# Tile by images in a diagonal LSTM kernel: another layout of the resident rows, other engines for the first statistics and the waiting rows' rounds

## The chip, the cores and the metric

The kernel runs on one core of one Trainium2 chip. A core has five engines that run their own instruction streams in order and meet at semaphores: TensorE (PE; PEld is its weight load), VectorE (DVE), ScalarE (ACT), GpSimd (POOL) and SyncE (SP), which here issues most of the DMA transfers. Times are device microseconds of one execution of the whole program; a kernel's time is the median of its runs.

## The reference

Input x has 16 images of 128 channels, 64 rows and 64 columns, in float32. What is computed is two residual layers, each on a group-normalised copy of its input (32 groups of 4 channels, statistics over the image):

```python
x = x + diagonal_lstm(gn(x), w_is, b_is, w_ss, b_ss)
x = x + quantum_conv(gn(x), pre_w, pre_b, q_weights, post_w, post_b)

# diagonal LSTM: row i is shifted right by i, and a scan runs over the 127 shifted columns
def step(h, c, ist):                       # h, c: [B, 128, 64 rows]
    gates = ist + w_ss[:, :, 0] @ h_of_row_above + w_ss[:, :, 1] @ h + b_ss
    o, f, i = sigmoid(gates[:384]); g = tanh(gates[384:])
    c = f * c + i * g
    return o * tanh(c), c
```

`ist` is `w_is @ gn(x) + b_is` on the shifted columns. Outside the image the shifted input is zero, but the state isn't: a row that hasn't begun still runs the recurrence on biases alone, and its state depends only on the step. The quantum layer is a fixed function per pixel: four angles from 128 channels, a simulated circuit of four qubits and two layers, four expectation values, and 128 channels out of these.

## The kernel before, in words

Channels lie on the 128 partitions throughout. The kernel has three stages.

**First stage.** The images are loaded and their statistics taken. Forty of the 64 rows of every image stay in SBUF in `ring`; the other 24 are loaded only for the statistics, into `rest` and `spare` tiles. `ring` is `[P, RING // ROWS, NB, BLOCK]`: blocks of four rows outermost, within a block the 16 images, within an image 256 elements. `rows(b)` loads image b into it by five transfers of 256 KB on SP's queue, `behind(b)` the remaining rows by three. `statistics(b, k)` is one bn_stats over 512 elements on DVE, eight for an image, `aggregated(b)` a bn_aggr of these. Interleaved with the images by a fixed ratio run 33 rounds (`inv_step`, `EARLY = 33`) that compute the state of rows that wait, one after the other: four products of `wsT` with the last state, broadcast to 128 columns (L195), four gate activations with a bias operand (L198), three small products and sums on Pool (L201 to L203), tanh and the product with the output gate on ScalarE (L205, L206). After each round stand two `keep` products (L178), whose results nobody reads. Pool's `turned` and `coefficients` compute the circuit's coefficients before the rounds. After the last round Pool copies the states into `hst` (L399, L400), TensorE computes the first gates' products (L405), three more `keep` products of 384 columns, and then `group_mean` (L143) turns the aggregated statistics into group means; the first normalisation and the scan follow.

**Scan.** Step t (160 steps, `NSTEP`) treats all 16 images along one diagonal of 32 rows; there are two bands of 32 rows, the second 65 steps later. In full steps an operation covers 512 columns: 32 rows of 16 images, held in two halves (q = 0, 1). A step does, on Pool: the copy to `edge` (L873), the differences of two rows' states (L620, L623), the addition of the state to the stored rows (`residual`, L632), and the normalised inputs of step t+2 (`normalised`, L570, L575, L580). TensorE has four wxT products on those inputs (L589) and the products with `wsT`, `w1T` and `w0T` (L768); the w0T products read the differences. DVE and ScalarE do the gates (L783, L787, L818) and the cell (L835 to L853). Where the others have time, DVE takes statistics of finished rows for the second normalisation (`statistics`, L720).

`diagonal` builds the access pattern into `ring`: a block's rows are addressed in pairs, and where the pairs don't align with a block, an operation is split into pieces. When the last column of a block of four rows is done, `residual` sends the block to `low` in DRAM by a transfer of 2 MB (L644), if its place is needed; when DVE has taken its statistics (`statistics`, called earlier in the step than that step's `residual`), the block's place is filled with four rows not yet loaded, by another of 2 MB (L727). There are six of each in the trace, and SP issues both. This stage's instructions are issued in the order in which they are written, under a manual schedule; the waits between them are derived by a framework from the addresses that each one reads and writes.

**Last stage.** Angles, sines, circuit products and outputs go by pieces of 512 pixels of an image; rows that are in `low` are read back. `rows_of(b, k)` gives a piece's place, `finish` adds the output to the rows and sends it out (L1072); in `ring`, two adjacent images share the place of the sum so that a transfer's source is in one stretch.

Of the kernel before, what the change touches and what calls it, by code (L numbers as in the profile page):

```python
# [27 lines left out]
EARLY = 33  # L28
FIRST = 8
# [52 lines left out]
def kernel(  # L82
# [27 lines left out]
    ring = const.tile([P, RING // ROWS, NB, BLOCK], F32, name="ring")  # L110
# [24 lines left out]

    def block(r):

        return (r + AHEAD if r < SLOTS else r - SLOTS) // ROWS
# [18 lines left out]
    with ExitStack() as scan:  # L157
# [29 lines left out]
        def inv_step(j, pool):  # L187


            ps = {}  # L190
            rhs = hinv[:, j : j + 1].to_broadcast([P, P])
            for g in ORDER:
                ps[g] = pool.tile([P, P], F32, name=f"inv_ps{j}_{g}", tag=f"inv{g}")
                w = wsT[:, g * 128 : (g + 1) * 128]
                nc.tensor.matmul(ps[g], lhsT=w, rhs=rhs, start=True, stop=True)  # L195
            ac = small.tile([P, 4], F32, name=f"inv_a{j}", tag="inv_a")
            for g in ORDER:
                nc.scalar.activation(ac[:, g : g + 1], ps[g][:, 0:1], FUNC[g], bias=bias[:, g : g + 1])  # L198
            ig = small.tile([P, 2], F32, name=f"inv_i{j}", tag="inv_i")
            c = cinv[:, j + 1 : j + 2]  # L200
            nc.gpsimd.tensor_mul(ig[:, 0:1], ac[:, GF : GF + 1], cinv[:, j : j + 1])  # L201
            nc.gpsimd.tensor_mul(ig[:, 1:2], ac[:, GI : GI + 1], ac[:, GG : GG + 1])
            nc.gpsimd.tensor_add(c, ig[:, 0:1], ig[:, 1:2])  # L203
            th = small.tile([P, 1], F32, name=f"inv_t{j}", tag="inv_t")
            nc.scalar.activation(th, c, AF.Tanh)  # L205
            nc.scalar.activation(  # L206
                hinv[:, j + 1 : j + 2], th, AF.Identity, scale=ac[:, GO : GO + 1]
            )
# [7 lines left out]
        with ExitStack() as prep:  # L216
# [27 lines left out]
            def rows(b):  # L244
                for k in ORDERED:
                    at = (2 * k * ROWS - AHEAD) * NW if k else SLOTS * NW
                    nc.sync.dma_start(
                        out=ring[:, 2 * k : 2 * k + 2, b, :],
                        in_=xv[b, :, at : at + CHUNK].rearrange("c (k n) -> c k n", n=BLOCK),
                    )  # L250
# [31 lines left out]
            def statistics(b, k):  # L282
                v = ring[:, 2 * k : 2 * k + 2, b, :] if k < 5 else rests[b][k - 5]
                nc.vector.bn_stats(stats[:, b, k, :], v)
# [6 lines left out]

            q3 = qw.rearrange("p (n a) -> p a n", a=3)
            ang = pp.tile([P, 2, 3, 8], F32, name="ang")
# [3 lines left out]
            def turned():  # L297
# [9 lines left out]
                nc.scalar.activation(trig, ang, AF.Sin, scale=TWO_PI)  # L307

            def coefficients():
                nc.gpsimd.tensor_mul(co[:, 0], trig[:, 0, 0, :], trig[:, 0, 2, :])  # L310
                nc.gpsimd.tensor_mul(co[:, 1], trig[:, 1, 0, :], trig[:, 0, 2, :])
                nc.gpsimd.tensor_mul(co[:, 2], trig[:, 0, 1, :], trig[:, 1, 2, :])
                nc.gpsimd.tensor_mul(co[:, 3], trig[:, 1, 1, :], trig[:, 1, 2, :])
                nc.gpsimd.tensor_scalar_mul(co[:, 4:8], co[:, 0:4], -1.0)
                nc.gpsimd.tensor_copy(cur[:, 0], expand)
                nc.gpsimd.memset(cur[:, 1], 0.0)
# [44 lines left out]
            coefficients()  # L361
# [9 lines left out]
            done = 0  # L371
            for b in range(NB):
                while b < NB - 1 and done * (NB - 1) < EARLY * (b + 1):
                    inv_step(done, ps_inv)
                    keep(ps_keep, "keep", ring[:, 2, b, 0:P])
                    keep(ps_keep, "keep", wsT[:, 0:P])
# [7 lines left out]
                    done += 1  # L384
                if b + 2 < NB:
                    rows(b + 2)
                if b + 1 < NB:
                    behind(b + 1)
                    for k in ORDERED:
                        statistics(b + 1, k)  # L390
                for k in (5, 6, 7):
                    statistics(b, k)
                aggregated(b)
# [111 lines left out]
        origin = ring[:, 0, 0, 0:1]  # L505
# [27 lines left out]
        def diagonal(t, band, q, j0, j1):  # L533


            j = j0
            while j < j1:
                odd = (j + AHEAD // 2 * (1 - band)) % 2
                n = 1 if odd or j + 1 == j1 else (j1 - j) // 2 * 2
                r = 2 * j + q + AHEAD * (1 - band)  # L540
                at = r // ROWS * NB * BLOCK + r % ROWS * NW + t - BAND * band - 2 * j - q
                dims = [[BLOCK, NB]]
                if n > 1:
                    dims = [[NB * BLOCK - ROWS, n // 2], [2 * NW - 2, 2]] + dims
                yield j, n, bass.AP(origin.tensor, origin.offset + at, [list(origin.ap[0])] + dims)
                j += n
# [5 lines left out]
        def over(v, n):  # L552
            if n == 1:
                return v
            return v.unsqueeze(1).unsqueeze(1).to_broadcast([P, n // 2, 2, NB])

        def by_pairs(v, q, j, n):
            v = v[:, q, j * NB : (j + n) * NB]
            return v if n == 1 else v.rearrange("p (k h i) -> p k h i", h=2, i=NB)

        def normalised(t):
# [4 lines left out]
            for band in range(2):  # L566
                s0, s1 = slots(t, band)
                j0, j1 = max(0, s0 - 1 + s0 % 2) // 2, (s1 + 1) // 2
                for j, n, x0 in diagonal(t, band, 0, j0, j1):
                    nc.gpsimd.tensor_sub(by_pairs(xn, 0, j, n), x0, over(mean1, n))  # L570
                j0, j1 = s0 // 2, s1 // 2
                uppers = diagonal(t, band, 0, j0, j1)
                for (j, n, lower), (_, _, upper) in zip(diagonal(t, band, 1, j0, j1), uppers):
                    of = over(mean1, n) if plain(t) else upper
                    nc.gpsimd.tensor_sub(by_pairs(xn, 1, j, n), lower, of)  # L575
# [49 lines left out]
        def residual(t, new, engine=nc.gpsimd):  # L625

            for band in range(2):
                s0, s1 = slots(t, band)
                for q in range(2):
                    j0, j1 = (s0 + 1 - q) // 2, (s1 + 1 - q) // 2  # L630
                    for j, n, x1 in diagonal(t, band, q, j0, j1):
                        engine.tensor_add(x1, x1, by_pairs(new, q, j, n))  # L632


            for g in range(NG2):
# [6 lines left out]
                if done == NW:  # L642
                    if 4 * g < NLOW:
                        nc.sync.dma_start(  # L644
                            out=low[:, :, 4 * g * NW : (4 * g + 4) * NW].rearrange("b c n -> c b n"),
                            in_=ring[:, block(4 * g)],
# [61 lines left out]
        def statistics(us):  # L708

            while waiting:  # L710
# [6 lines left out]
                v = ring[:, q, i, :].rearrange("p (r w) -> p r w", w=NW)[:, :, w0:w1]  # L717
                if w1 - w0 == NW:
                    v = ring[:, q, i, :]
                nc.vector.bn_stats(stats[:, i, g - FIRST * k, :], v)  # L720
                if i == NB - 1:
# [4 lines left out]
                    if 4 * g < NLOW:  # L726
                        nc.sync.dma_start(  # L727
                            out=ring[:, q],
# [147 lines left out]
        def low_rows(queue, n, v):  # L876
            b, k = n // NT, n % NT
            of = low[b, :, k * CHUNK : (k + 1) * CHUNK]
            queue.dma_start(out=v, in_=of if len(v.shape) == 2 else of.rearrange("p (k n) -> p k n", n=BLOCK))
# [4 lines left out]
        with tc.manual_schedule():  # L884
# [26 lines left out]
            v = ring[:, block(NH - ROWS)].rearrange("p i (r w) -> p i r w", w=NW)[:, :, :, NW - STRIP :]  # L911
# [17 lines left out]

# [46 lines left out]
    def rows_of(b, k):  # L976
        if k < NT:
            return lows[NT * b + k]
        q = block(2 * ROWS * k)
        return ring[:, q : q + 2, b, :]  # L980

    def half(v, c):
# [3 lines left out]
        return v[:, c] if len(v.shape) == 3 else v[:, c * BLOCK : (c + 1) * BLOCK]  # L986
# [70 lines left out]
    def finish(b, h, po, c=None):  # L1057
        for j in range(4):
# [3 lines left out]
            to = place = v  # L1062
            if c is not None:
                o, to = o[:, c * BLOCK : (c + 1) * BLOCK], x1
            elif k >= NT:


                q = block(2 * ROWS * k)
                to = ring[:, q, b - 1 : b + 1, :] if b % 2 else ring[:, q + 1, b - 2 : b, :]
                y = y.rearrange("p (k n) -> p k n", n=BLOCK)  # L1070
                place = to.rearrange("p k n -> p (k n)")
            nc.vector.scalar_tensor_tensor(to, y, b_out, x1, ALU.add, ALU.add)  # L1072
            nc.sync.dma_start(out=o, in_=to if c is not None else place)
            if c is None or c == 1 and k < NT:
                places.append(place)
# [96 lines left out]
```

## Time and profile before

| | us |
|---|---|
| runs of the kernel before | 1411.84, 1413.09, 1413.08 |
| median | 1413.08 |
| span of the profiled execution | 1411.1 |
| the median over that span | 2.0 |
| first stage, up to group_mean (L143) | 0 to 100.97 |
| scan | about 104 to 1287 |
| last stage | about 1287 to 1411 |
| busy: TensorE, DVE, ScalarE, Pool | 1354.3, 979.7, 777.0, 921.1 |
| moved by DMA | 107.06 MB |

The profile is of one execution. Busy times are of the engine, not of its queue: an engine that waits at a semaphore is not busy. A timeline line has the start in us, the duration (of several joined instructions together), the engine, the line of the kernel, the operation with its output and inputs by tile name, shape and count, and in brackets the idle time ahead of it with what ended it. A line of a table of stretches has the stretch and its length, then for PE, PEld, DVE, ACT and POOL the busy us with the number of instructions, the granted TensorE clock, the DMA share and GB/s.

### The profile page before, as it was taken

What the parts mean: (1) busy time and instruction counts of PE and PEld (TensorE: products, weight loads), DVE (VectorE), ACT (ScalarE), POOL (GpSimd) and SP (SyncE); (2) the same over time, 40 slices, a digit from 0 to 9 for tenths busy, and PEclk for the clock granted to TensorE, in tenths of its full rate; (3) what the DMA queues carried; (4) which work ended last, traced back from release to release, by engine and by line L of the source; (5) the groups of instructions that cost most, each with busy time, mean ns of one, the idle gap of its engine ahead of it and who ended that gap; (6) DMA issues with size and microseconds to landing.
All of it is one profiled execution on the core that took longest, in us unless ns stands there. A gap on an engine that the chain in (4) does not pass through costs nothing. (4 is left out here: it accounts for less than half of the span.)

```text
span 1411.1 us, 20316 instructions
## 1 busy us (share of the span) xinstructions
PE 1354.3 (96%) x6046; PEld 966.1 (68%) x6046; DVE 979.7 (69%) x2541; ACT 777.0 (55%) x1852; POOL 921.1 (65%) x1823
## 2 busy tenths in 40 slices
PE   6778999999999999999999999999999999999995
PEld 4658988777777777666677777776666777886332
DVE  7983565566665666787777776666665566876996
ACT  4545666555555555555555555555555566554331
POOL 4226788777777777777788876777777677773300
PEclk9999999999999999999999999999999999999997
DMA  9980000000000000133333100000000000004999
GB/s 326 367 287 2 1 2 0 1 1 1 0 1 1 0 1 1 60 120 120 120 120 120 60 1 1 0 1 1 1 1 0 1 1 1 2 30 143 386 404 350
DMA packets 78925, 107.06 MB, mean 76 GB/s; under 512 B 5552, under 2 KB 53712, under 8 KB 78816
## 3 DMA queue, kind: packets, MB, share of 16 engines
q1 hardware_dynamic: 74176, 94.39, 19.2%
q0 software_dynamic: 3408, 10.58, 2.0%
q8 instruction: 48, 0.79, 0.2%
q10 hardware_dynamic: 1232, 0.80, 0.2%
q14 instruction: 61, 0.50, 0.1%
HBM read 59.61 MB, written 46.14 MB: 75 GB/s over the span
## 5 line engine op out<-in xcount | busy, mean ns | idle before, releaser
L589 PE MATMUL ps<-spare,wxT 128*128 128x512 f32 (+18 forms) x1280 | 480.6, 519 | 0.0
L783 DVE TENSOR_TENSOR ps<-ps,both 128x256 f32<-128x256 f32 (+9 forms) x536 | 219.5, 411 | 304.4 <-PE ps L768 302.6
L787 ACT ACTIVATE ps<-ps,bias 128x512 f32<-128x512 f32 (+23 forms) x480 | 279.4, 583 | 221.7 <-DVE ps L783 185.2
L768 PE MATMUL ps<-spare,w1T 128*128 128x256 f32 (+16 forms) x1272 | 346.6, 354 | 8.8 <-DVE spare L744 4.6
L589 PEld LDWEIGHTS ps<-spare,wxT 128*128 128x128 f32 x1280 | 231.8, 191 | 172.6 <-issue 155.5
L768 PE MATMUL ps<-spare,w0T 128*128 128x256 f32 (+16 forms) x1272 | 343.8, 352 | 0.8 <-POOL spare L623 0.8
L818 ACT COPY both<-ps 128x256 f32<-128x256 f32 (+9 forms) x536 | 189.8, 356 | 181.1 <-PE ps L768 161.4
L632 POOL TENSOR_TENSOR ring<-ring,spare 128x256 f32<-128x256 f32 (+8 forms) x487 | 247.7, 540 | 30.8 <-DVE stats L720 20.7
L768 PEld LDWEIGHTS ps<-spare,w1T 128*128 128x128 f32 x1272 | 230.4, 190 | 35.8 <-DVE spare L853 6.8
L768 PEld LDWEIGHTS ps<-spare,wsT 128*128 128x128 f32 x1088 | 195.5, 190 | 80.5 <-DVE spare L853 29.9
L768 PE MATMUL ps<-spare,wsT 128*128 128x256 f32 (+14 forms) x1088 | 243.8, 366 | 2.4 <-DVE spare L853 1.2
L768 PEld LDWEIGHTS ps<-spare,w0T 128*128 128x128 f32 x1272 | 230.3, 190 | 22.2 <-POOL spare L623 1.0
L580 POOL TENSOR_TENSOR spare<-spare,rstd 128x512 f32<-128x512 f32 (+10 forms) x160 | 171.0, 1069 | 14.8 <-DVE rstd L154 2.3
L575 POOL TENSOR_TENSOR spare<-ring 128x256 f32<-128x256 f32 (+8 forms) x213 | 147.2, 701 | 0.0
L847 ACT ACTIVATE g<-cst 128x256 f32<-128x256 f32 (+20 forms) x320 | 103.2, 369 | 64.2 <-DVE cst L846 63.3
L570 POOL TENSOR_TENSOR spare<-ring,mean 128x16 f32<-128x16 f32 (+8 forms) x247 | 130.9, 540 | 8.3 <-DVE mean L144 7.2
L853 DVE TENSOR_TENSOR spare<-g,ps 128x256 f32<-128x256 f32 (+17 forms) x319 | 105.7, 368 | 43.3 <-ACT g L847 40.8
L623 POOL TENSOR_TENSOR spare<-spare 128x240 f32<-128x240 f32 (+9 forms) x136 | 102.7, 755 | 29.3 <-DVE spare L853 25.5
L787 ACT ACTIVATE g<-ps,bias 128x512 f32<-128x512 f32 (+20 forms) x160 | 97.4, 609 | 26.9 <-DVE ps L783 20.7
L873 POOL COPY spare<-spare 128x16 f32<-128x16 f32 x64 | 21.1, 330 | 134.2 <-DVE spare L853 134.2
L846 DVE TENSOR_TENSOR cst<-cst,ps 128x256 f32<-128x256 f32 (+20 forms) x320 | 104.6, 368 | 5.5
L843 DVE TENSOR_TENSOR ps<-ps,g 128x512 f32<-128x512 f32 (+20 forms) x160 | 95.1, 595 | 19.0 <-ACT g L787 18.8
(370 smaller groups left out, 1097.3 us busy)
## 6 DMA issues: line engine op xcount, KB each, us to landing
out_dram<-ring SPq DMA_DIRECT2D x93, 256.0 KB, 5.3
ring<-in_x_dram SPq DMA_DIRECT2D x80, 256.0 KB, 5.6
low<-ring SPq DMA_DIRECT2D x6, 2048.0 KB, 7.5
ring<-in_x_dram SPq DMA_DIRECT2D x6, 2048.0 KB, 8.3
spare<-in_x_dram SPq DMA_DIRECT2D x27, 256.0 KB, 5.5
rest<-in_x_dram SPq DMA_DIRECT2D x21, 256.0 KB, 5.6
ring<-low POOLq DMA_DIRECT2D x18, 256.0 KB, 6.7
low<-low POOLq DMA_DIRECT2D x14, 256.0 KB, 5.9
```

The costliest lines, as they stand in the source:

```text
L570: nc.gpsimd.tensor_sub(by_pairs(xn, 0, j, n), x0, over(mean1, n))
L575: nc.gpsimd.tensor_sub(by_pairs(xn, 1, j, n), lower, of)
L580: nc.gpsimd.tensor_mul(v, v, r)
L589: nc.tensor.matmul(ps[g][:, :, a:b], lhsT=wxT[:, g * 128 : (g + 1) * 128], rhs=xns[t % 2][:, :, a:b], start=t > 0, stop=True, skip_group_c ...
L632: engine.tensor_add(x1, x1, by_pairs(new, q, j, n))
L768: nc.tensor.matmul(out, lhsT=w[:, g * 128 : (g + 1) * 128], rhs=rhs, start=False, stop=True, skip_group_check=True,)
L783: nc.vector.tensor_add(v, v, both[g][:, a:b])
L787: nc.scalar.activation(to[:, :, a:w], ps[g][:, :, a:w], FUNC[g], bias=bias[:, g : g + 1])
L818: nc.scalar.copy(both[g][:, a:b], ps[g][:, 0, a:b])
L846: nc.vector.tensor_add(c[:, q], c[:, q], ig[:, q])
L847: nc.scalar.activation(th[:, q, a:w], c[:, q], AF.Tanh)
L853: nc.vector.tensor_mul(new[:, q, a:v], th[:, q, a:v], act[GO][:, q, a:v])
```

## The change

The tile `ring` gets the image as its outermost index: `[P, NB, RING * NW]`. An image's forty rows are one stretch; a diagonal is one operation for each half and band, no longer pieces; an image is loaded by three transfers of 4, 4 and 2 KB per partition instead of five; the sum of the last stage is written in its own place.

In the first stage, the first 512 elements' statistics of images 1 to 8 are taken by two ScalarE passes with an accumulator (`moments_of`: sum of differences to the first element, sum of their squares). The aggregation of images 1 to 12 goes to Pool, as a generator of small operations for four images at a time (`gathering`), of which one portion is issued after each round; what is left follows after the last round. Images 0 and 13 to 15 keep bn_aggr. A round's products have 32 columns instead of 128; the bias is brought by a product of the identity with the broadcast bias, which starts the accumulation, and the activations have no bias operand. The two `keep` products of a round become one of 384 columns. The sines and coefficients of the circuit move behind the rounds and the rest of the aggregation.

```diff
-    ring = const.tile([P, RING // ROWS, NB, BLOCK], F32, name="ring")
+    ring = const.tile([P, NB, RING * NW], F32, name="ring")
...
+    def place(r):
+
+        return (r + AHEAD if r < SLOTS else r - SLOTS) * NW
+
     def block(r):
 
-        return (r + AHEAD if r < SLOTS else r - SLOTS) // ROWS
+        return ring[:, :, place(r) : place(r) + BLOCK]
...
-        def inv_step(j, pool):
+        def inv_step(j, pool, ident):
             ps = {}
-            rhs = hinv[:, j : j + 1].to_broadcast([P, P])
+            rhs = hinv[:, j : j + 1].to_broadcast([P, THIN])
             for g in ORDER:
-                ps[g] = pool.tile([P, P], F32, name=f"inv_ps{j}_{g}", tag=f"inv{g}")
+                ps[g] = pool.tile([P, THIN], F32, name=f"inv_ps{j}_{g}", tag=f"inv{g}")
+                of = bias[:, g : g + 1].to_broadcast([P, THIN])
+                nc.tensor.matmul(ps[g], lhsT=ident, rhs=of, start=True, stop=False)
+            for g in ORDER:
                 w = wsT[:, g * 128 : (g + 1) * 128]
-                nc.tensor.matmul(ps[g], lhsT=w, rhs=rhs, start=True, stop=True)
+                nc.tensor.matmul(ps[g], lhsT=w, rhs=rhs, start=False, stop=True)
...
-                nc.scalar.activation(ac[:, g : g + 1], ps[g][:, 0:1], FUNC[g], bias=bias[:, g : g + 1])
+                nc.scalar.activation(ac[:, g : g + 1], ps[g][:, 0:1], FUNC[g])
...
             def rows(b):
-                for k in ORDERED:
-                    at = (2 * k * ROWS - AHEAD) * NW if k else SLOTS * NW
+                for r, n in ((0, SLOTS // 2), (SLOTS // 2, SLOTS // 2), (SLOTS, AHEAD)):
                     nc.sync.dma_start(
-                        out=ring[:, 2 * k : 2 * k + 2, b, :],
-                        in_=xv[b, :, at : at + CHUNK].rearrange("c (k n) -> c k n", n=BLOCK),
+                        out=ring[:, b, place(r) : place(r) + n * NW],
+                        in_=xv[b, :, r * NW : (r + n) * NW],
                     )
...
+            def moments_of(b):
+                at = place(SLOTS)
+                v, x0 = ring[:, b, at : at + CHUNK], ring[:, b, at : at + 1]
+                junk = ps_small.tile([P, CHUNK], F32, name=f"junk{b}", tag="small")
+                for k, func in enumerate((AF.Identity, AF.Square)):
+                    nc.scalar.activation(
+                        junk, v, func, bias=x0, scale=-1.0, accum_out=sums1[:, k, b : b + 1]
+                    )
+
+            def gathering(b0):
+                b1 = b0 + GATHER
+                pair = [P, GATHER, 2]
+                means, inners = entries[:, b0:b1, :, 1], entries[:, b0:b1, :, 2]
+                s1, s2 = (sums1[:, k, b0:b1] for k in range(2))
+                if b0 in apart:
+                    x0 = ring[:, b0:b1, place(SLOTS)].unsqueeze(2).to_broadcast(pair)
+                    nc.gpsimd.tensor_scalar_mul(s1, s1, -1.0 / CHUNK)
+                    nc.gpsimd.tensor_add(means[:, :, 0:2], s1.unsqueeze(2).to_broadcast(pair), x0)
+                    yield
...
+                def total(to, v):
+                    n = 8
+                    while n > 1:
+                        nc.gpsimd.tensor_add(gathered[:, :, 0:n], v[:, :, 0:n], v[:, :, n : 2 * n])
+                        v, n = gathered, n // 2
+                        yield
+                    nc.gpsimd.tensor_add(to.unsqueeze(2), v[:, :, 0:1], v[:, :, 1:2])
+                    nc.gpsimd.tensor_scalar_mul(to, to, 1.0 / 16)
+                    yield
+
+                yield from total(m, means)
+                nc.gpsimd.tensor_sub(gathered, means, m.unsqueeze(2).to_broadcast([P, GATHER, 16]))
+                nc.gpsimd.tensor_mul(gathered, gathered, gathered)
+                yield
+                nc.gpsimd.tensor_scalar_mul(within, inners, 1.0 / BLOCK)
+                nc.gpsimd.tensor_add(gathered, gathered, within)
+                yield
+                yield from total(var, gathered)
...
+
+            def coefficients():
                 nc.scalar.activation(trig, ang, AF.Sin, scale=TWO_PI)
-
-            def coefficients():
+                nc.scalar.activation(warm, shift, AF.Sqrt)
...
             biases()
-            coefficients()
...
             for b in range(NB):
                 while b < NB - 1 and done * (NB - 1) < EARLY * (b + 1):
-                    inv_step(done, ps_inv)
-                    keep(ps_keep, "keep", ring[:, 2, b, 0:P])
-                    keep(ps_keep, "keep", wsT[:, 0:P])
+                    inv_step(done, ps_inv, ident)
+                    some()
+                    keep(ps_keep, "keep", wsT[:, 0 : 3 * P])
...
+                if b in apart:
+                    moments_of(b)
...
-                        statistics(b + 1, k)
+                        if k or b + 1 not in apart:
+                            statistics(b + 1, k)
...
-                aggregated(b)
+                if b in (0, *range(13, NB)):
+                    aggregated(b)
+                if b in (5, 9, 13):
+                    behind_pool.append(gathering(b - GATHER))
+            for later in behind_pool:
+                for _ in later:
+                    pass
+            coefficients()
...
         def diagonal(t, band, q, j0, j1):
...
+            r = 2 * j0 + q + AHEAD * (1 - band)
+            at = r * NW + t - BAND * band - 2 * j0 - q
+            dims = [[2 * NW - 2, j1 - j0], [RING * NW, NB]]
+            return bass.AP(origin.tensor, origin.offset + at, [list(origin.ap[0])] + dims)
...
-                    for j, n, x1 in diagonal(t, band, q, j0, j1):
-                        engine.tensor_add(x1, x1, by_pairs(new, q, j, n))
+                    if j0 < j1:
+                        x1 = diagonal(t, band, q, j0, j1)
+                        engine.tensor_add(x1, x1, by_pairs(new, q, j0, j1))
...
                             out=low[:, :, 4 * g * NW : (4 * g + 4) * NW].rearrange("b c n -> c b n"),
-                            in_=ring[:, block(4 * g)],
+                            in_=block(4 * g),
...
                         nc.sync.dma_start(
-                            out=ring[:, q],
+                            out=q,
                             in_=xv[:, :, (RING + 4 * g) * NW : (RING + 4 * g + 4) * NW].rearrange(
```

## The prediction, made before the changed kernel had run

> **What bounds the kernel now.** I read the forty slices first, then stretches of the scan, then the order of time in one scan step, and last the first hundred microseconds.
>
> ```profile
> PE   6778999999999999999999999999999999999995
> DVE  7983565566665666787777776666665566876996
> POOL 4226788777777777777788876777777677773300
> PEclk9999999999999999999999999999999999999997
> ```
>
> ```profile
> 700.00:800.00 100.00, 100.00 (x371) 69.76 (x370) 71.82 (x184) 58.94 (x128) 81.08 (x184) 1.00 0.32 106
> ```
>
> A slice is 35 us. DVE leads the first three, TensorE the scan, DVE the end. In the stretch 700 to 800 TensorE is busy all 100 us at full clock and Pool 81: the scan runs at TensorE's pace, so whatever delays a product there is added to the time. What Pool still has spare shows in step 70 (start, us, engine, line):
>
> ```profile
> 610.12 0.20 POOL L873 COPY spare<-spare 128x16 f32<-128x16 f32 x1 [1.65 <-DVE spare L853]
> 610.46 0.86 POOL L623 TENSOR_TENSOR spare<-spare 128x240 f32<-128x240 f32 x1
> 611.29 2.34 POOL L632 TENSOR_TENSOR ring<-ring,spare 128x16 f32<-128x16 f32 x7
> 613.59 0.67 POOL L570 TENSOR_TENSOR spare<-ring,mean 128x192 f32<-128x192 f32 x1
> 615.82 1.27 POOL L580 TENSOR_TENSOR spare<-spare,rstd 128x512 f32<-128x512 f32 x1
> 618.73 0.20 POOL L873 COPY spare<-spare 128x16 f32<-128x16 f32 x1 [1.64 <-DVE spare L853]
> ```
>
> ```profile
> 612.46 0.59 PE L768 MATMUL ps<-spare,w0T 128*128 128x256 f32 x2
> ```
>
> ```profile
> 613.59 0.38 SPq L727 DMA_DIRECT2D ring<-in_x_dram  x1
> 620.79 0.37 SPq L644 DMA_DIRECT2D low<-ring  x1
> ```
>
> The period is 8.61 us (610.12 to 618.73). Pool idles 1.65 of it; its differences end at 611.32 and the first w0T product, which reads them, starts at 612.46, so its lead is 1.14 us more. Behind the differences stand, in Pool's order, the adds to the ring (residual, L632) and the two-steps-ahead normalisation. The page puts the 2 MB reload of a block (L727) at 8.3 us to landing, nearly a whole step, and the copy to low (L644) at 7.5. Neither is waited for in step 70: Pool's only waits from 560 to 780 are 41.0 us for DVE, 25 times.
>
> In the first stage a round of the waiting rows takes 2.39 us, 33 times (hinv starts at 88.98, then 91.38):
>
> ```profile
> 88.98 0.30 ACT L206 ACTIVATE hinv<-inv_t,inv_a 128x1 f32<-128x1 f32 x1
> 89.33 0.97 PEld L195 LDWEIGHTS inv_ps<-hinv,wsT 128*128 128x128 f32 x8 [0.66 <-ACT hinv L206]
> 89.85 0.93 ACT L198 ACTIVATE inv_a<-inv_ps,bias 128x1 f32<-128x1 f32 x4 [0.58 <-PE inv_ps L195]
> 91.38 0.29 ACT L206 ACTIVATE hinv<-inv_t,inv_a 128x1 f32<-128x1 f32 x1
> ```
>
> It is a chain of latencies; its last hinv is written at 94.06. DVE is busy 19.8 of every 20 us there and ends its last aggregation at 100.87; group_mean follows at 100.97. So DVE sets the end of this stage: what follows the rounds, the first gates' products, is over at 96.4.
>
> **What the Trainium skill says.** "DMA: Bandwidth & Descriptors", Anatomy of one DMA: DMA engines do not wait on semaphores, the issuing sequencer does, and about 2 us of a transfer are fixed. So a Pool that waits for a landing waits the whole 8.3 us; the trace agrees on the size (2.1 MB at 350 to 390 GB/s plus 2 is near 8). "TensorE: Matmul & The Clock Gate", LDWEIGHTS: the load's cost goes with the stationary's columns. The trace agrees: fp32 products of 16 and of 128 columns both start 0.22 us apart, so a narrow product is no cheaper to issue. Same page, Part 1: an idle window of about 3.4 us halves the clock until a busy one. The trace has one: sparse products from 99.5 to 102.9, then a granted clock of 0.50 from 103.0 to 106.3. "ScalarE: Activation LUTs", What ACT_TABLE_LOAD costs: a pointer operand adds about 93 ns; here L198 with its bias takes 263 ns, L205 without 203.
>
> **The change, part by part.**
>
> *Ring by images, in the scan.* A diagonal then steps over all images at 10 KB, so the address range of one access spans nearly the whole ring, other blocks' rows included. In the built program's order of instructions with their waits, residual's first add now waits for a block transfer in twelve steps: in steps 70, 74, 78, 82, 86, 90 for the reload issued in that same step, in 68, 72, ... 88 for the copy to low issued the step before. None of these is a true dependency, and the program before has none of them. Behind that add on Pool are the normalisation and the next differences, and for those waits TensorE.
>
> First reload: issue 613.59; landing +8.3; four merged adds instead of seven 1.85 (L570's 64 and 192 columns at 0.34 and 0.67 put 0.17 on a piece, three pieces fewer than 2.34); normalisation 3.5 (0.67+0.84+0.34+0.40+1.27); L873 to L623 1.2. The differences are there 14.9 us after the issue; TensorE wants them at 612.46+8.61 = 621.07, 7.5 after. Stall 7.4. The other five are issued earlier in their step (785.08 against a product at 794.03: 8.95), stall 5.95 each. Sum 7.4 + 29.8 = **37 us**. From below: if landing is 7.5 and Pool catches up half a microsecond, 30. From above, if the reload lands at 9.3: 43.
>
> Each stall is longer than one idle window, so the clock should be half for some 3.4 us after it: 1.7 us lost, six times 10; not each gap holds a full window, I take **9** (0 to 12).
>
> The low copies land 7.5 after the issue, 628.3 in the first case, when Pool gets to the add (8.61 x 2 after 611.3 is 628.5): 0, at most 1 each. The add also waits for the step's statistics in three steps of four from 68 to 98, some 2.2 us each (DVE's group ends at 613.5, Pool is ready at 611.3); Pool's 1.65 idle, 0.5 saved and 1.14 lead cover it: 0, up to 7 us in all. Merged adds shorten Pool, which has time left: 0, and below nothing too no more than that, since TensorE is full.
>
> *First stage.* DVE loses 8 x 0.69 (images 1 to 8) + 12 x 0.372 (aggregations) = 10.0 us and would end near 92. Loads in 4 KB pieces instead of 1 KB: records of 1, 2 and 4 KB take 47, 86 and 159 ns, some 10% less for an image, so the load doesn't hold DVE up. But the cover changes hands:
> - A round's latency falls by 0.18 to 2.2 (0.06 to 0.09 without the pointer; 0.09 by a narrow last pass, since L143's result of 16 columns is read 0.43 us after its product starts, L195's of 128 after 0.52), but TensorE now issues eight products (8 x 0.22) and a 384-column filler (0.6 to 0.7) in it: 2.4, as before. Eight rounds have two ScalarE passes over 512 columns put ahead (about 0.58 each as L787, 0.6 exposed: 5 us). The first round starts 1.9 us earlier, since Sin, coefficients and memsets no longer stand ahead. Last hinv 92.5 to 97, I take 95.
> - Behind the last round Pool still has 27 of the aggregation's small dependent steps (0.2 to 0.4, mean 0.31: 8.4 us), the seven coefficient steps moved there (1.25), three copies (0.5); then TensorE's eight first products (1.8) and three fillers (2.1) stand ahead of group_mean. Sin's table load (1.28) is hidden by the 27 steps. Total 14.1 after the last Pool step of a round, 0.5 before hinv: 94.5 + 14.1 = 108.6.
> So group_mean is at 108.6 against 100.97: **+8** (+5 to +10; DVE's end alone would give -8).
>
> *Last stage.* Same bytes and counts; a sum into 2-D rather than 3-D places takes 741 against 743 ns: 0.
>
> Sum against the profiled 1411.1: +37 +9 +8 = 1465; the median of the runs is 2.0 above the profile, so **1467**. About 0.2% (2.8 us) is what a measurement can tell from no change.
>
> **Rivals.**
> - *The likeliest*, 1467 (1448 to 1484): chance 0.60.
> - *Stalls as said, but DVE and the loads set the first stage's end* (Pool's small steps nearer 0.2 and fit between rounds): 1413 + 46 - 8 = 1451. For it: DVE's 10 us are real. Against: 27 steps stand after the last round in Pool's order. 0.14.
> - *The waits are absorbed*: the transfers land before Pool needs them. Then the scan costs 0 to 10 and the first stage 8: 1425. For it: such a wait costs only what exceeds the 3.3 us of spare and lead. Against: 8.3 us to landing on six reloads. 0.17.
> - *Faster*: the waits cost nothing and DVE's end at 92 to 93 is the stage's end: 1413 - 8 = 1405. It decides once an average round takes below about 2.05 us and landing below about 3 us after issue; the trace shows 2.39 and 8.3. 0.06.
> - *No net effect*: no stall, and the first stage ends as now: 0.03.
>
> The predicted time is the likeliest's, 1467. The range 1424 to 1482 takes most of it, the second, and the upper half of the third. Faster 0.06, same 0.03, slower 0.91.
>
> **What would show it.** Right: Pool's residual waits on DMA in steps 70, 74, ... 90, six holes of 6 to 7 us in TensorE, 34 us apart or a little more, each followed by half clock; group_mean at 106 to 111 behind Pool's gathering. Wrong: TensorE full from 560 to 900, or group_mean before 100.

## The result, and the profile after

The changed kernel takes 1534.75 us (median; 1533.66 to 1547.27) against 1412.82 (the median of four runs of the kernel before): a ratio of 1.0888 (95% interval 1.085 to 1.0926), 122 us slower. The forecast was 1467, with a range to 1482. The direction was right, and so was the mechanism in the scan; the first stage was off by 66 us. (Single executions of four kernels took longer than the others, by some 12 us for the changed kernel and the one with its first stage alone and by 65 to 69 us for the filler kernel and the combined one; the text says which is meant.)

Of the page's slices, now 38 us each, the clock's row shows what the forecast had not:

```profile
PE   7999699999999999998888889999999999999996
PEclk9555799999999999999999999999999999999998
```

The stretches of the first stage (length, then busy us and count of PE, PEld, DVE, ACT, POOL, then clock, DMA share, GB/s):

```profile
20.00:40.00 20.00, 19.66 (x116) 16.59 (x116) 14.94 (x24) 10.94 (x55) 3.49 (x19) 0.80 1.00 377
40.00:60.00 20.00, 20.00 (x77) 17.27 (x77) 17.45 (x29) 8.53 (x36) 2.69 (x14) 0.50 1.04 404
80.00:100.00 20.00, 20.00 (x80) 17.57 (x79) 14.70 (x26) 8.18 (x34) 3.24 (x17) 0.50 0.59 230
120.00:140.00 20.00, 20.00 (x76) 17.19 (x76) 0.00 (x0) 5.40 (x27) 3.78 (x20) 0.50 0.00 0
```

From 31.9 to 159 TensorE is at half clock and, but for short gaps, always busy; then it waits 9.29 us for Pool, and the clock is full again at 171.8. Its instructions in 20 us fall from 116, in a stretch of which 12 us are at full clock, to 77. The kernel before was busy for less than four fifths of such a stretch, at full clock:

```profile
40.00:60.00 20.00, 15.76 (x102) 12.45 (x101) 19.79 (x34) 11.95 (x51) 5.21 (x27) 1.00 1.07 364
```

DVE and the loads are done by 95 (DVE's last aggregation starts at 94.62), and then the core does nothing but rounds and what Pool has left. One round at full clock, and one at half:

```profile
25.64 0.97 PE L201 MATMUL inv_ps<-bias,ident 128*128 128x32 f32 x8
26.45 1.06 PE L204 MATMUL inv_ps<-hinv,wsT 128*128 128x32 f32 x8
27.34 0.89 PE L184 MATMUL I-365_366<-wsT 128*128 128x384 f32 x2
28.07 0.97 PE L201 MATMUL inv_ps<-bias,ident 128*128 128x32 f32 x8
```

```profile
60.43 1.76 PE L201 MATMUL inv_ps<-bias,ident 128*128 128x32 f32 x8
62.00 1.90 PE L204 MATMUL inv_ps<-hinv,wsT 128*128 128x32 f32 x8
63.71 1.63 PE L184 MATMUL I-671_672<-wsT 128*128 128x384 f32 x2
65.13 1.75 PE L201 MATMUL inv_ps<-bias,ident 128*128 128x32 f32 x8
```

From start to start of L201 that is 2.43 us and 4.70. The last hinv is written at 158.6, and group_mean, at 100.97 before, comes here (DVE's line, which reads its result, says how long DVE had waited):

```profile
174.76 0.40 PE L149 MATMUL gm<-mv,wide_sb 128*128 128x16 f32 x2
175.20 0.17 DVE L150 TENSOR_SCALAR mean<-gm 128x16 f32<-128x16 f32 x1 [80.20 <-PE gm L149]
```

The waits in the scan are as forecast. Waits of Pool and of TensorE between 560 and 1000 (us in all, times, longest):

```profile
POOL ring L707 <- DMA ring<-in_x_dram: 59.1, 6, 10.5
POOL ring L707 <- DVE stats L795: 26.4, 17, 2.4
```

```profile
PE ps L843 <- POOL spare L697: 37.0, 6, 7.0
```

And the first of the six holes (the time in which TensorE stands still), in TensorE's timeline and in stretches of it:

```profile
700.97 1.22 PE L843 MATMUL ps<-spare,w0T 128*128 128x256 f32 x2 [7.03 <-POOL spare L697]
701.99 1.06 PE L843 MATMUL ps<-spare,w1T 128*128 128x256 f32 x2
```

```profile
694.00:695.00 1.00, 0.00 (x0) 0.00 (x0) 0.00 (x0) 0.00 (x0) 0.32 (x1) 1.00 0.00 0
702.00:703.00 1.00, 1.00 (x4) 0.81 (x3) 0.43 (x1) 0.23 (x1) 1.00 (x4) 0.50 0.00 0
706.00:707.00 1.00, 1.00 (x3) 0.38 (x2) 1.00 (x3) 0.76 (x2) 0.18 (x1) 1.00 1.05 347
```

By milestones: the scan's first wxT product starts at 178.47 instead of 104.45 (+74.0); from there to the first product on the sums of the second normalisation it is 1227.4 us instead of 1178.3 (+49.1); what follows takes 127.7 instead of 128.4. Together 122.4, the difference of the two spans.

### The profile page after: what moved, and what is told of

The parts are those of the page before. It is cut to its first block, busy times and chain, and to the rows that moved or that the text cites. A ratio compares the mean times of both kernels' runs of the same rounds, so it can differ in the third digit from the quotient of the medians.

```text
span 1533.5 us, 20475 instructions
## 1 busy us (share of the span) xinstructions
PE 1450.9 (95%) x6244; PEld 1051.2 (69%) x6244; DVE 965.7 (63%) x2521; ACT 782.6 (51%) x1886; POOL 898.6 (59%) x1653
## 4 chain that ended last, share of the span: by engine, by line
PE 72%; DVE 4%; DMA 3%; POOL 3%; issue 1%; ACT 1%; DVEq 0%; ACTq 0%; SPq 0%; POOLq 0%
PE ps L843 41%; PE ps L663 24%; DMA ring<-in_x_dram 3%; PE po_None L1121 3%; PE theta_None L1070 2%; PE am_None L1099 1%; POOL ring L707 1%; DVE spare L928 1%; DVE stats L795 1%; DVE ps L918 1%; POOL spare L654 1%; DVE ps L858 1%; POOL spare L649 1%; DVE cst L921 0%; POOL spare L644 0%
## 5 line engine op out<-in xcount | busy, mean ns | idle before, releaser
L843 PE MATMUL ps<-spare,w0T 128*128 128x256 f32 (+16 forms) x1272 | 352.4, 359 | 37.6 <-POOL spare L697 37.6
L843 PE MATMUL ps<-spare,w1T 128*128 128x256 f32 (+16 forms) x1272 | 352.8, 359 | 8.8 <-DVE spare L819 4.8
L707 POOL TENSOR_TENSOR ring<-ring,spare 128x256 f32<-128x256 f32 (+15 forms) x375 | 231.2, 643 | 106.6 <-DMA ring<-in_x_dram 59.1
L843 PEld LDWEIGHTS ps<-spare,w0T 128*128 128x128 f32 x1272 | 234.4, 194 | 62.6 <-POOL spare L697 40.2
L843 PEld LDWEIGHTS ps<-spare,w1T 128*128 128x128 f32 x1272 | 234.9, 194 | 37.6 <-DVE spare L928 6.6
L649 POOL TENSOR_TENSOR spare<-ring 128x256 f32<-128x256 f32 (+13 forms) x165 | 139.6, 846 | 0.0
L922 ACT ACTIVATE g<-cst 128x256 f32<-128x256 f32 (+20 forms) x320 | 102.9, 368 | 63.6 <-DVE cst L921 63.1
L644 POOL TENSOR_TENSOR spare<-ring,mean 128x256 f32<-128x256 f32 (+15 forms) x191 | 122.6, 642 | 7.1 <-DVE mean L150 7.0
L910 DVE TENSOR_TENSOR cst<-cst,ps 128x512 f32<-128x512 f32 (+20 forms) x160 | 92.8, 580 | 16.7 <-POOL spare L687 9.6
```

Of the source, the lines that this page charges most:

```text
L644: nc.gpsimd.tensor_sub(by_pairs(xn, 0, j0, j1), x0, over(mean1, j1 - j0))
L649: nc.gpsimd.tensor_sub(by_pairs(xn, 1, j0, j1), lower, of)
L707: engine.tensor_add(x1, x1, by_pairs(new, q, j0, j1))
L843: nc.tensor.matmul(out, lhsT=w[:, g * 128 : (g + 1) * 128], rhs=rhs, start=False, stop=True, skip_group_check=True,)
```

## The experiments

Theory A: two costs that have nothing to do with each other, false waits in the scan (ring by images) and a half clock in the first stage (the new rounds). Theory B: the layout or its larger loads cause the half clock as well. Within A, A1 says that the clock follows how many columns the array is given; A2 blames weight loads or a gap near 31 us.

**The two halves of the change.** The ring's layout, loads and diagonals alone, and the first stage's edits alone (on the ring by blocks).

```diff
 # ring alone, against the changed kernel
-                    inv_step(done, ps_inv, ident)
-                    some()
-                    keep(ps_keep, "keep", wsT[:, 0 : 3 * P])
+                    inv_step(done, ps_inv)
+                    keep(ps_keep, "keep", ring[:, b, 2 * BLOCK : 2 * BLOCK + P])
+                    keep(ps_keep, "keep", wsT[:, 0:P])
...
 # first stage alone, against the changed kernel
-    ring = const.tile([P, NB, RING * NW], F32, name="ring")
+    ring = const.tile([P, RING // ROWS, NB, BLOCK], F32, name="ring")
```

> The ring by images alone (the ring's layout, its loads in three transfers, the diagonal in one piece); statistics, rounds, fillers and coefficients as before. Theory A (two separate costs: stalls of the scan by false waits, and a half clock made by the new rounds): full clock in the first stage, group_mean near 101 or a little earlier; six holes in TensorE of 6 to 7 us for Pool, about 37 us, each followed by 3.4 us at half clock; time about 1413 + 48 = 1461. Theory B (the half clock of the first stage comes from the layout or its larger loads): half clock from about 32 us on here too, group_mean well behind 110, time above 1490.

> The first stage's changes alone (narrow products with the bias product, one filler of 384 columns, ScalarE's statistics, Pool's aggregation, coefficients behind), with the ring by blocks of rows as before. Theory A: half clock from about 32 us on, rounds of 4.7 us, group_mean near 175, no hole in TensorE in the scan, time about 1413 + 74 = 1487. Theory B: full clock, group_mean at 106 to 115, time 1420 to 1427.

Ring alone: 1461.61 us, ratio 1.0348 (1.0331 to 1.0366); TensorE's waits in the scan are

```profile
PE ps L765 <- POOL spare L619: 35.1, 6, 6.6
```

and group_mean starts at 100.62, with the rounds at full clock. First stage alone: 1485.7 us, ratio 1.0536 (1.0498 to 1.0574), with

```profile
60.00:80.00 20.00, 20.00 (x79) 17.57 (x80) 19.43 (x30) 7.77 (x32) 3.09 (x16) 0.50 1.08 372
```

and group_mean at 174.09; its scan takes 1178.0, as before the change. The two add up: 48.9 + 73.0 = 121.9 of 122. Theory B falls.

**What lowers the clock.** Wider products in the rounds, and the sparse stretch taken away:

```diff
-THIN = 32
+THIN = 128
```

> The changed kernel with 128 columns instead of 32 in the rounds' products (bias products included); all else as changed. Theory A1 (the clock follows how many columns the array takes in: per round now (8 x 32 + 384)[...] in 2.43 us[...], 44%; before (4 x 128 + 2 x 128)[...] in 2.39, 53%; here [...]over 90%): clock 1.00 through the first stage, rounds 2.4 to 2.6, group_mean near 114, time about 1475. Theory A2 (the clock falls because weight loads fill the rounds, or because of a gap in TensorE near 31 us, whatever the width): half clock as in the changed kernel, time about 1535.

```diff
-                    elif done > 4 and between:
-                        between.pop(0)()
...
             coefficients()
+            for later in between:
+                later()
```

> The changed kernel with the two small weight preparations (angle and output weights) taken out of the rounds and put behind them; they stand at 30.6 and 35.3 us, where the clock falls. Theory A2 in its gap form: without that sparse stretch the clock stays at 1.00, group_mean near 114, time about 1475. Theory A1: 44% of the array is too little or at the edge, so the clock falls in some other round, at the latest in those that wait for ScalarE's two passes, and stays at half: group_mean 160 to 180, time 1520 to 1540.

With 128 columns: 1479.12 us (ratio 1.0471, 1.0455 to 1.0487), full clock in the rounds with the same weight loads and as many products, group_mean at 117.40 (the forecast was 114, and 1475 for the time; behind the rounds, while TensorE waits for Pool, the clock is at 0.50 from 105.1 to 115.3):

```profile
60.00:80.00 20.00, 19.78 (x144) 17.31 (x143) 19.10 (x33) 11.44 (x56) 7.26 (x37) 1.00 1.04 407
```

Without the sparse stretch: 1535.93 us, no gain; the clock falls one microsecond later, in the middle of an ordinary round (the stretch between these two has a clock of 0.88):

```profile
31.00:32.00 1.00, 0.91 (x9) 0.80 (x8) 1.00 (x2) 0.50 (x2) 0.21 (x2) 1.00 1.08 416
33.00:34.00 1.00, 1.00 (x3) 0.69 (x3) 0.94 (x3) 0.60 (x4) 0.39 (x2) 0.50 1.04 420
```

So neither the weight loads nor that gap is the cause: with the same products and loads, widening them from 32 to 128 columns alone brings the full clock back. How many are needed was tried from both sides:

```diff
 # the changed kernel
                     keep(ps_keep, "keep", wsT[:, 0 : 3 * P])
+                    keep(ps_keep, "keep", wsT[:, 0 : 2 * P])
```

> The changed kernel with its 32-column rounds, and behind each round's filler of 384 columns a second one of 256. Theory A1 (array's share of a window decides): (8 x 32 + 640)[...]; a round is TensorE's 16 weight loads and streams, some 2.43 + 0.43 = 2.86 us, so 52% at full clock, as much as before the change: clock 1.00, group_mean near 15 + 33 x 2.86 + 5 + 16 = 130, time about 1491. Theory A3 (it is the narrow products themselves, or the share of time in weight loads, that the clock follows): half clock again, rounds about 5.5 us, time about 1560.

This kernel was executed twice: 1499.9 us with a mean granted clock of 0.980, and 1568.82 with 0.931. The profile is of the longer one: full clock until 42, and then

```profile
60.00:80.00 20.00, 19.76 (x64) 14.54 (x64) 19.27 (x33) 6.96 (x28) 1.81 (x10) 0.50 1.04 408
```

Each of the two executions lies some 9 us above what one of the theories gave (1491 and 1560): the kernel seems to stand on the edge, as far as two executions can tell. That the shorter one kept its full clock is read from its time and its mean clock, since it has no trace. My 52% was wrong, though: a round at full clock took 3.19 us (22.67 to 25.86) and not 2.86, so the share is 47%. Why the second filler adds 0.76 us, where its columns take 0.43, wasn't tested. The other side, on the kernel before with 32-column rounds, bias operands and the coefficients behind the rounds, with fillers of 640 and of 384 columns:

```diff
 # against the kernel before; the last line is left out in the second kernel
-            rhs = hinv[:, j : j + 1].to_broadcast([P, P])
+            rhs = hinv[:, j : j + 1].to_broadcast([P, THIN])
...
-                    keep(ps_keep, "keep", ring[:, 2, b, 0:P])
-                    keep(ps_keep, "keep", wsT[:, 0:P])
+                    keep(ps_keep, "keep", wsT[:, 0 : 3 * P])
+                    keep(ps_keep, "keep", wsT[:, 0 : 2 * P])
```

> The kernel before (ring by blocks) with the same first stage as the combined version: 32 columns with bias operands, fillers of 384 + 256, coefficients behind. Theory A: full clock, the rounds end near 90, but the load by 1 KB runs ends near 97.5 and DVE at 100.9 as before, so group_mean stays at 100 to 101: time as before within 1.5 us. Rival (the rounds' end is what sets group_mean in the kernel before): 3 to 5 us faster.

> The same as the block version, with the second filler of 256 columns taken out: nothing else differs. Theory A1: (4 x 32 + 384)[...] in 2.3 us, 37%: half clock, rounds of 3.0 to 3.3 us, group_mean 118 to 126, time 1430 to 1438. Rival (bias products, ScalarE's passes or Pool's aggregation, all absent here, are what lowers the clock): full clock, time as the block version.

With 640: 1413.19 us (ratio 1.0009, 1.0000 to 1.0017), full clock, group_mean at 100.48, the last hinv 1.6 us earlier than before and of no use, since DVE still ends at 100.4. With 384: 1429.17 us (1.0123, 1.0104 to 1.0141), half clock from 25 us on, rounds of 2.98 us, group_mean at 116.92, all a little below the forecast:

```profile
40.00:60.00 20.00, 20.00 (x67) 14.84 (x68) 19.53 (x34) 10.30 (x41) 3.84 (x20) 0.50 1.07 362
```

One filler of 256 columns is all that differs. A column of an fp32 product takes 1.69 ns at full clock (eight products of 256 columns in the 3.45 us from 612.03 to 615.48), which gives the share of a round in which columns stream (a round's length is taken where the clock is still full):

| kernel | columns in a round | round, us | share | clock in the rounds |
|---|---|---|---|---|
| 32 columns, filler 384 | 512 | 2.31 | 37% | half |
| changed | 640 | 2.43 | 45% | half |
| changed, filler 640 | 896 | 3.19 | 47% | full or half |
| before | 768 | 2.39 | 54% | full |
| 32 columns, filler 640 | 768 | 2.31 | 56% | full |
| changed, 128 columns | 1408 | 2.43 | 98% | full |

So in these rounds the line runs somewhere between 47% and 54%. That TensorE stands still isn't what counts: in the kernel before it waited 0.47 us in each round and kept its clock, in the changed kernel's rounds it didn't wait and lost it.

**The tail behind the rounds.** On the 128-column version, bn_aggr stays on DVE for all images, Pool only turns ScalarE's sums into DVE's form, and the coefficients go behind the copies of the states.

```diff
-                if b in (0, *range(13, NB)):
+                if b not in apart:
                     aggregated(b)
-                if b in (5, 9, 13):
+                if b in (5, 9):
                     behind_pool.append(gathering(b - GATHER))
+                if b in (9, 13):
+                    for i in range(b - 8, b - 4):
+                        aggregated(i)
```

> The changed kernel with 128-column rounds (full clock) in which the tail behind the rounds is taken away: bn_aggr on DVE for all images (Pool only turns ScalarE's sums into DVE's form, in the rounds), and sines and coefficients behind the copies of the states. Theory A (the tail is serial: 27 small Pool steps, seven coefficient steps): group_mean 105 to 106 instead of 117.4, time about 1467. Rival (the tail lies beside TensorE's fillers, or DVE's aggregations at the end cost as much): group_mean 114 to 117, time 1476 to 1479.

1468.1 us (1.0399, 1.0376 to 1.0421), group_mean at 105.92 instead of 117.40. Pool's steps there had taken from 99.89 to 110.28, so the tail lay on the path.

**How long a false wait is.** The ring version with the reload's issue moved behind the step's normalisation, then also halved. `reloaded` issues what `statistics` has put on a list, whole in the first kernel and by 8 images in the second:

```diff
             if t + 2 < NSTEP:
                 normalised(t + 2)
+            reloaded()
```

> The ring by images alone, with the 2 MB reload issued after the same step's normalisation instead of behind the last statistics. Theory A (Pool's next ring access waits until landing, whatever it needs; what counts is how much of the 8.4 us lies beside Pool's work that doesn't touch the ring, plus Pool's idle time and lead): issue 3.3 us later, and the wait falls on the next step's residual instead of this one's; Pool's differences are ready 6.55 + 8.4 us after an issue at 616.9, 631.9, against 612.46 + 2 x 8.61 = 629.7: stalls of about 2.3, six times 14 us, too short for half clock: time about 1428. Rival (a wait only moves: each reload still costs 6 us and a half clock): about 1461.

> As the late reload, in two halves of 8 images (1 MB), the first issued a step earlier, as soon as its images' statistics are done; each after its step's normalisation. Theory A: 1 MB at 380 GB/s plus 2 us lands after 4.8 us, so the differences are ready at 616.9 + 4.8 + 6.55 = 628.3 against 629.7: no stall in TensorE; what is left is the copies to low (0 to 1 us each): time 1413 to 1419. Rival (twelve waits instead of six, each with a landing time that hardly falls with the size): stalls of 2 us twelve times, 1435 to 1440.

Late: 1424.15 us (1.0089, 1.0071 to 1.0107), TensorE's waits for Pool 9.4 us in place of 35.1, and no half clock. In halves: 1416.08 (1.0030, 1.0019 to 1.0042); 1 MB lands after 5.4 us.

```profile
PE ps L774 <- POOL spare L619: 3.8, 6, 0.8
```

Pool now also waits for the copies to low (13.0 us, four times), mostly in its spare time. The false wait is still there, eleven times for reloads; what went is the part of it that didn't fit beside work that leaves the ring alone.

**A version that draws on both.**

```diff
 # both, against the ring version: the rounds of the kernel with fillers of 640, and
-                if done == NW:
-                    if 4 * g < NLOW:
...
+                if done in (NW, NW + 1) and 4 * g < NLOW:
+                    i0 = (done - NW) * NB // 2
+                    i1 = i0 + NB // 2
...
+                if 4 * g < NLOW:
+                    reloads.append((g, i))
...
 # the second alone, ahead of group_mean
-                keep(ps_small, "small", v[:, 0 : 3 * P])
+                keep(ps_small, "small", v[:, 0:P])
```

> A version that draws on both findings. Ring by images; the reload goes out in the steps' own portions (6, 6 and 4 images, as their statistics are done), each after its step's normalisation; the copy to low in two halves in two steps. Rounds with 32 columns, bias as an operand (no bias product), fillers of 384 + 256 columns; coefficients behind the copies of the states; statistics and aggregation on DVE as before. Theory A: array share of a round (4 x 32 + 640)[...] in 2.3 us, 56%: full clock; last hinv near 90, DVE's end (94.1 with the halves) sets group_mean at 95 to 96 instead of 99.9; TensorE's waits of 3.8 us for Pool nearly gone: time about 1409 (1407 to 1412), 2 to 5 us under the kernel before. Rival (a threshold of the clock above 56% for narrow products, or waits that only multiply with the portions): half clock and 1440, or 1416 to 1422.

> The combined version with the three fillers ahead of group_mean cut from 384 to 128 columns each; nothing else differs. In the block version, which has the same rounds, the last hinv is written at 92.4; the first gates' products end 2.3 us later at 94.7, and fillers of 0.9 each would put group_mean at 97.4, later than the 95 to 96 that was expected of the combined version. Theory (these fillers stand on the path): group_mean at 95.6 to 96.2, 1.5 us less: time 1409 to 1410.5. Rival (without them TensorE is too sparse there, and the half clock that the kernel before has from 103.0 to 106.3 comes earlier or stays longer): group_mean earlier, but the scan's first products at half clock, time 1411 to 1415. If an execution's rounds begin at half clock they stay there: 1475.

The first took 1411.35 us, ratio 0.9996 (0.9988 to 1.0004): no difference. One of its fourteen executions, the profiled one, took 1476.23: there the rounds stayed at half clock from the first to the last (4.27 us a round). Where the expected gain went is read from the other kernels with these rounds: the last hinv is at 92, not 90, and three fillers that nobody reads stood ahead of group_mean. The second differs in their width alone: 1409.39 us, ratio 0.9980 (0.9973 to 0.9988), faster than the kernel before, and all of its 16 executions lie within 2 us.

```profile
94.81 0.39 PE L185 MATMUL I-1369_1370<-rest,wsT 128*128 128x128 f32 x2
96.35 0.40 PE L150 MATMUL gm<-mv,wide_sb 128*128 128x16 f32 x2
```

```profile
PE ps L777 <- DVE spare L610: 1.7, 4, 0.7
```

group_mean is at 96.35 against 100.97, while the scan is 1.2 us longer than before (99.86 to 1279.39 is 1179.5), though TensorE waits no more for Pool from 560 to 1000; what made it longer is open. Its rounds are those of the combined version, so a start at half clock isn't excluded, only not seen.

## Why the prediction was right and wrong

- *The six stalls*: 37 us forecast, 37.0 measured; first hole 7.4 forecast, 7.03 measured, the others about 6.0. The profile's landing time, Pool's row times and the product that waits were enough, once the built program's waits had been read. Two small misses offset each other in the first hole: the reload took about 0.5 us longer (8.8 us is the median), and TensorE wanted the differences 8.2 us after the issue, not 7.5. (The section of the Trainium skill named there for the fixed 2 us, "DMA: Bandwidth & Descriptors", Anatomy of one DMA, describes transfers issued by GpSimd; these came from SP, and the sum rests on the trace's 8.3.)
- *Half clock after them*: 9 us forecast. The clock is 0.50 for 6.8 us at each of the six holes (697.5 to 704.3 at the first), and TensorE works in 25.8 of these 41.0 us, which costs an estimated 12.9. The scan lost 49.1, of which 37.0 are waits; this accounts for the other 12. The forecast took 3.4 us of work at half clock for a hole and not quite all of the six; it was 4.3 on average, at each of them.
- *Waits for statistics and low, merged adds*: 0 forecast. Pool waited 26.4 us for statistics from 560 to 1000, and none of it shows in TensorE's waits. Right.
- *DVE's end at 92, loads 10% shorter*: 94.99, and 404 against 370 GB/s. The number is near by luck, for the reason was wrong. DVE's last aggregation in the kernel before, with the ring alone, with the first stage alone and in the changed kernel:

```profile
100.50 0.37 DVE L287 BATCH_NORM_AGGREGATE mv<-stats 128x2 f32<-128x48 f32 x1
94.79 0.37 DVE L292 BATCH_NORM_AGGREGATE mv<-stats 128x2 f32<-128x48 f32 x1
100.30 0.37 DVE L292 BATCH_NORM_AGGREGATE mv<-stats 128x2 f32<-128x48 f32 x1
94.62 0.37 DVE L295 BATCH_NORM_AGGREGATE mv<-stats 128x2 f32<-128x48 f32 x1
```

  The larger loads alone bring 5.7 us with all of DVE's work still there; taking 10 us of work from DVE brings 0.2 on either ring. "So the load doesn't hold DVE up" was the mistake: DVE waited 4.3 us for loads between 10 and 102 before the change, and 10.6 after it. This end decided nothing here, since group_mean came later for other reasons.
- *The rounds*: **this is the step that failed.** "TensorE now issues eight products and a 384-column filler in it: 2.4, as before" is right at full clock (2.43), and so was the reading that a narrow product costs as much to issue. What was missing is that a narrow product gives the array less to do, and that the clock follows this. The prediction had a half-clock stretch of the kernel before in hand and named the page of the Trainium skill on it ("TensorE: Matmul & The Clock Gate", Part 1: a monitor of how busy TensorE has been sets its clock), but used it only where TensorE idles. That section speaks of idle and busy windows; here TensorE had no idle time in the full-clock rounds and lost its clock all the same. (The stretch of the kernel before wasn't an idle window either: TensorE was busy for 2.07 us between 99.4 and 103.0.) Rounds of 4.70 us instead of 2.4 put the last hinv at 158.6 instead of 95: 63.6 of the 66 us.
- *The rounds at full clock*: the case with 128 columns shows that the forecast of 108.6 was too early without the half clock, too. Its last hinv is at 100.5 and its group_mean at 117.40. The start is part of it: the round was to begin 1.9 us earlier, but the second hinv came at 20.66, after 19.00 before the change.
- *The tail*: 13.6 us from the last hinv forecast, 16.1 measured; the eight first products took 3.5 us at half clock (168.49 to 171.95) instead of 1.8. The case with 128 columns had Pool's part at 10.4, against 10.2 in the sum.
- *The range* ended at 1482, since none of its cases had a first stage that is slower than its instructions at full clock. The rival for a faster kernel had asked for a round below 2.05 us; no kernel came there.

## What to carry to other kernels

A busy TensorE isn't always a fast one: before making products narrower, or cutting fillers, count the columns that stream in a stretch, because the clock followed them here, and a full busy row hid the loss. A layout in which one strided access spans the whole tile can make each transfer into it a wait for the next access, whatever that one needs, and costs the part of the landing time that isn't beside work elsewhere; read the built program's waits, then move the issue, or split it, before giving up the layout. Before work is taken from the engine that ends a stage last, ask whether its loads would hold it at the same place; and look at what then stands in its place in the queues of the others, here fillers and small dependent steps.

## What was unexpected of the hardware

- The clock has a memory. Rounds with 56% of the time streaming ran at full clock in two traces, those of the filler of 640 and of the second combined kernel. In the combined version's long execution the clock hadn't risen ahead of them, and the same rounds, in which columns then stream for 61% of the time at the slower rate (768 columns of 3.37 ns in 4.27 us), didn't bring it back in over 130 us. The eight back-to-back products of 128 columns behind them did so within 5 us (156.7 to 161.5), and after the holes of the scan TensorE was back at full clock after 3.1 to 6.0 us of work.
- It takes its time to fall: the changed kernel's rounds ran at 45% and full clock for 13 us before it went to half at 31.9.
- The clock's column can be wrong at the start: in the combined version's long execution it shows 1.00 throughout the rounds, where fillers of 384 columns take 1.63 us as at half clock elsewhere (0.89 at full); the first record of the clock in that trace is at 161.5. The first round of the changed kernel has 1.63 under a 1.00, too. Durations tell it, not the column. The mean clock on record misleads in the same way: the changed kernel's execution of 1547.27 us has 0.983, the three shorter ones 0.937 to 0.939. It has no trace; rounds at half clock from the start would fit (five to six of them lie between 18.3 and 31.9 us, and 2.27 us more for each is an estimated 11 to 14), but this isn't shown.
